# A convolution and attention block on one core: softmax without a shift, with a checked sum and a shifted pass behind a branch

## The chip, the core and the metric

The kernel runs on one core of one Trainium2 chip. Time is the device time of one execution in microseconds (us). Engines are named as the profile names them: PE (TensorE), DVE (VectorE), ACT (ScalarE), POOL (GpSimd), SP (SyncE, which here issues transfers).

## What is computed

Four images of 384 channels and 48 x 48 pixels (N = 2304 tokens) pass through one block, in float32:

```
local = batch_norm(depthwise_conv_7x7(x))
x_norm = layernorm(x tokens)
q, k, v = split(x_norm @ qkv_w.T + qkv_b)         # 8 heads of width 48
q = q + layernorm(local tokens)
attn = softmax(q @ k.T * 48 ** -0.5)
out = x + (attn @ v) @ proj_w.T + proj_b
```

The weights of qkv are normal with variance 1/384; all gains are 1 and all biases 0.

## The kernel before

**Tiles.** An image's tokens form 6 groups (g) of 384, that is 8 image rows or 3 blocks of 128. The 8 heads form 4 pairs (p). In a pair the even head lies on partitions 0 to 47, the odd one on 64 to 111. Row 48 (112) of a query tile holds minus the maximum of that query's scores and row 48 of a key tile holds 1, so the score product, over 49 rows, gives shifted scores.

**Attention** (`attention`, L399) takes one pair of one group of queries and walks over 18 blocks of 128 keys. For each: two score products into `s` (L423, two buffers of PSUM), one exponential of 128 x 768 on ACT into `pt` (L431, three buffers), and, one step later, two products with the values into the accumulator `o` (L409). The values carry a column of ones, so `o` holds the sum of the weights in one more row. There is one buffer for `o`. At the end of the pair ACT and then DVE copy its two halves to `osb` (L442, L443, two buffers), and the next pair can't write `o` until both have.

**Maxima** (`max_part`, L292). The maximum has to be there before the scores are shifted, so while a pair is attended to, the next pair's scores are computed a first time: 36 products of 128 queries by 384 keys (L301), each reduced by DVE to one maximum a query (L309), then a transpose (L314) and two small transfers into row 48 of the query tile (L319). `attention` pulls one step of it a key block. The first pair of an image has its maxima made before its loop.

**Work in between.** Everything else is written as generators whose steps are taken from a queue, `behind`, by `advance(units)` after each key block, five steps at a time. At p = 0 of a group the next group's `q_part` is appended: 147 convolution taps on DVE (L258 and L262, three chunks of 128 channels, each tap a multiply-add onto `acc`, which has one buffer), two layer norms (transposes on PE L145 and L183, statistics L149 and L150, a power on POOL L153, the scaling L157, copies on ACT), four query projections (L199) and four joins with the local part (L280, L285). Behind a pair follows `pair_output` (L335 transposes, L341 reciprocal of the sum, L342 quotient), behind a group `group_output` (L356, L366 projection, L373 residual, then the transfer out). `finish()` empties the queue; it is called before the last pair of a group, as the next group's maxima need its queries. In the last group of an image the queue also gets the first key/value part (`kv_part`: L145, L183, L199, L221) and the first queries of the next image; the other five key/value parts stand between the images, followed by `finish()`.

**Order.** The text is only a priority. A scheduler lays each engine's instructions in one fixed order by a model of their times, and fills an engine's free time with what comes later in the text if its inputs are there. On the chip each engine then goes through its list in that order.

Of the kernel before, what the change touches and what calls it, by code (L numbers as in the profile page):

```python
# [11 lines left out]
ALU = mybir.AluOpType  # L12
AX = mybir.AxisListType

P = 128
NH = 8  # heads
HD = 48  # head width
KS = 7  # convolution window
LN_EPS = 1e-6
BN_EPS = 1e-5  # L20
RG = 8  # image rows in a token group
AHEAD = 1  # key/value groups of the next image that are made ahead


# Two heads share a tile: the even one lies on partitions 0..47 and the odd one on 64..111.
# Row 48 (112) is one more term of the score product: 1 on the key side, minus the row's
# maximum on the query side, so that the product is already the shifted score.
@with_exitstack
def conv_attention(
    ctx: ExitStack,  # L30
    tc: tile.TileContext,
    x: bass.AP,  # [B, C, N]
    conv_w: bass.AP,  # [128, CC, 49]
    bn: bass.AP,  # [128, 4, CC] gamma, beta, mean, var
    ln: bass.AP,  # [128, 2, CC] gamma, beta
    ln_pair: bass.AP,  # [2, 48, 2, 4]
    qk_b: bass.AP,  # [2, 48, 2, 4]
    v_b: bass.AP,  # [1, C]
    qkv_wT: bass.AP,  # [C, 3C]
    proj_wT: bass.AP,  # [C, C]  # L40
    proj_b: bass.AP,  # [128, CC]
    out: bass.AP,  # [B, C, N]
):
# [4 lines left out]
    CC = C // P  # L48
    G = RG * W  # tokens of a group
    NG = N // G  # L50
    NB = G // P  # blocks of 128 tokens in a group
    NP = NH // 2
    KB = N // P
    SCALE = float(HD) ** -0.5
    HA = HD + 1
    KP = 64 + HA

    const = ctx.enter_context(tc.tile_pool(name="const", bufs=1))
# [8 lines left out]

# [1 line left out]
    x_tiles = {}  # L69
# [31 lines left out]
    for j in range(2):  # L101
# [3 lines left out]
        nc.scalar.dma_start(out=qkb[r + HD : r + HA, 1, :], in_=ones)  # L105
    # The query's bias takes the local term's beta as well.
    nc.vector.tensor_add(qkb[:, 0, :], qkb[:, 0, :], ln_p[:, 1, :])
# [14 lines left out]

    # The batch norm goes into the convolution's weights and a shift.
    inv = const.tile([P, CC], F32, tag="inv", name="inv")
# [8 lines left out]

# [1 line left out]
    def normalized(src, dst):  # L135
        """src(c, blk): channels by tokens. dst(blk): where a block's normalized tokens go,
        [128 tokens, heads, 48]."""
        xt = work.tile([P, NB, C], F32, tag="xt", name="xt")
# [28 lines left out]
    def x_normalized(b, g):  # L167
        """The layer norm of x, channels by tokens."""
        xs = x_tiles[b]
# [65 lines left out]

    # The centre of the window is first, as it alone covers every pixel.
    taps = sorted(range(KS * KS), key=lambda t: t != KS * KS // 2)
# [54 lines left out]
    def max_part(b, g, p):  # L292
        """Minus the maximum of each row of scores, into the query's last row."""
        q = queries[b, g][p]
# [32 lines left out]
    def pair_output(b, g, p, osb):  # L327
        """Divides by the sums, tokens by channels."""
        if p == 0:
            outputs[b, g] = work.tile([P, NB, NH, HD], F32, tag="ao", name="ao", bufs=1)  # L330
        ao = outputs[b, g]
        tp = psum()
        ot = tp[:, :G].rearrange("p (t h d) -> p t h d", t=NB, h=2)
        for blk in range(NB):
            nc.tensor.transpose(  # L335
                tp[:, blk * P : blk * P + KP],
                osb[0:KP, blk * P : (blk + 1) * P],
                ident[0:KP, 0:KP],
            )
        rden = work.tile([P, NB, 2, 1], F32, tag="rden", name="rden")  # L340
        nc.vector.reciprocal(rden, ot[:, :, :, HD:HA])  # L341
        nc.vector.tensor_mul(  # L342
            ao[:, :, 2 * p : 2 * p + 2, :],
            ot[:, :, :, 0:HD],
            rden.to_broadcast([P, NB, 2, HD]),
        )
        yield
# [32 lines left out]

# [1 line left out]
    behind = deque()  # work to be spread over the attention's loop  # L382

# [15 lines left out]
    def attention(b, g, p, ahead, units):  # L399
        """ahead: the next pair's max_part, or None."""  # L400
        q = queries[b, g][p]
# [16 lines left out]
        for kb in range(KB):  # L418
            s = ps_s.tile([P, 2, 512], F32, tag="s", name="s")
            blk = kb % NB  # L420
            for j in range(2):
                r = 64 * j
                nc.tensor.matmul(  # L423
                    s[:, j, :G],
                    lhsT=keys[b, kb // NB][r : r + HA, p, blk * P : (blk + 1) * P],
                    rhs=q[r : r + HA, :],
                    start=True,
# [24 lines left out]
    for b in range(B):  # L452
        for _ in max_part(b, 0, 0):
            pass
        for g in range(NG):
            for p in range(NP):
                ahead = None
                if p < NP - 1:
                    ahead = max_part(b, g, p + 1)
                elif g < NG - 1:  # L460
                    finish()
                    ahead = max_part(b, g + 1, 0)
# [7 lines left out]
                if p == NP - 1 and g == NG - 2 and b < B - 1:  # L470
                    load_x(b + 1)
                attention(b, g, p, ahead, 5)
        if b < B - 1:
            for ga in range(AHEAD, NG):
                behind.append(kv_part(b + 1, ga))
        finish()


# [49 lines left out]
```

## Time and profile before

| | |
|---|---|
| median of 3 runs | 5941.53 us (5937.75 to 5945.82) |
| span of the profiled execution | 5940.5 us |
| PE, DVE, ACT, POOL busy | 5593.6, 3993.9, 1791.8, 172.9 us |
| max product L301 on PE, reductions L309 on DVE | 1894.3 and 1783.6 us |
| convolution taps L262 on DVE | 1873.0 us |
| mean granted clock of PE | 0.955 |

The profile gives no other time of the profiled execution than its span. A busy time is the time in which at least one instruction of the engine or group ran; matmuls overlap. In a row of the timeline stand start, duration, engine, line, operation, operands and count, and in brackets the idle time before it and what ended it. `x4` in a row of PE is two float32 matmuls, since each is recorded as two instructions. The granted clock is a share of full speed; in this trace it is either 1 or 0.5 at any moment.

### The profile page before, as it was taken

What the parts mean: (1) busy time and instruction counts of PE and PEld (TensorE: products, weight loads), DVE (VectorE), ACT (ScalarE), POOL (GpSimd) and SP (SyncE); (2) the same over time, 40 slices, a digit from 0 to 9 for tenths busy, and PEclk for the clock granted to TensorE, in tenths of its full rate; (3) what the DMA queues carried; (4) which work ended last, traced back from release to release, by engine and by line L of the source; (5) the groups of instructions that cost most, each with busy time, mean ns of one, the idle gap of its engine ahead of it and who ended that gap; (6) DMA issues with size and microseconds to landing.
All of it is one profiled execution on the core that took longest, in us unless ns stands there. A gap on an engine that the chain in (4) does not pass through costs nothing.

```text
span 5940.5 us, 63623 instructions
## 1 busy us (share of the span) xinstructions
PE 5593.6 (94%) x24720; PEld 2349.8 (40%) x24720; DVE 3993.9 (67%) x8263; ACT 1791.8 (30%) x2545; POOL 172.9 (3%) x325
## 2 busy tenths in 40 slices
PE   6999999999899999999989999999998999999999
PEld 4433333334343333333434333333344433333343
DVE  6795786784738668668563866866855487687543
ACT  2123233223222322322322233233332223323333
POOL 1000000000000000000000000000000000000000
PEclk9799999999999999999989999999999999999999
DMA  1000000000000000000000000000000000000000
GB/s 42 1 1 5 5 1 5 5 25 5 5 1 1 5 5 1 5 5 25 5 5 1 1 5 5 1 5 5 25 5 5 1 2 3 5 2 4 5 5 5
DMA packets 21646, 35.33 MB, mean 6 GB/s; under 512 B 8992, under 2 KB 19808, under 8 KB 19808
## 3 DMA queue, kind: packets, MB, share of 16 engines
q1 hardware_dynamic: 13248, 28.61, 1.3%
q10 hardware_dynamic: 8096, 2.65, 0.2%
q8 instruction: 194, 3.18, 0.2%
q14 instruction: 108, 0.88, 0.0%
HBM read 16.80 MB, written 14.16 MB: 5 GB/s over the span
## 4 chain that ended last, share of the span: by engine, by line
PE 58%; DVE 37%; ACT 2%; POOL 2%; issue 1%; DMA 0%; ACTq 0%; DVEq 0%; POOLq 0%
DVE acc L262 22%; PE s L423 16%; PE o L409 15%; PE pm L301 14%; DVE part L309 9%; PE pm L199 6%; PE pm L366 2%; PE pm L221 2%; DVE st L149 2%; POOL rs L153 1%; PE pm L183 1%; DVE osb L443 1%; DVE xt L157 1%; PE pm L145 1%; DVE lt L157 0%
## 5 line engine op out<-in xcount | busy, mean ns | idle before, releaser
L309 DVE TENSOR_REDUCE part<-pm 128x1 f32<-128x384 f32 x3456 | 1783.6, 551 | 1250.8 <-PE pm L301 1243.4
L431 ACT ACTIVATE pt<-s 128x768 f32<-128x768 f32 x1728 | 1398.2, 811 | 3021.2 <-PE s L423 3019.3
L301 PE MATMUL pm<-k,q 48*128 48x384 f32 x6912 | 1894.3, 513 | 55.6 <-DVE part L309 36.9
L262 DVE SCALAR_TENSOR_TENSOR acc<-x,cw,acc 128x368 f32<-128x368 f32 (+9 forms) x3456 | 1873.0, 582 | 21.1
L423 PE MATMUL s<-q,k 49*128 49x384 f32 x6912 | 1662.9, 553 | 2.7 <-DMA q<-negT 2.7
L409 PE MATMUL o<-pt,v 128*49 128x384 f32 x6912 | 1521.0, 518 | 9.6 <-ACT pt L431 9.4
L301 PEld LDWEIGHTS pm<-k,q 48*128 48x128 f32 x6912 | 850.2, 193 | 778.4 <-DVE part L309 315.1
L423 PEld LDWEIGHTS s<-q,k 49*128 49x128 f32 x6912 | 579.4, 192 | 993.3 <-PE pm L301 490.8
L409 PEld LDWEIGHTS o<-pt,v 128*49 128x49 f32 x6912 | 311.4, 124 | 984.6 <-issue 743.3
L199 PE MATMUL pm<-xnT,w_qk 128*128 128x384 f32 x1152 | 443.3, 534 | 17.8 <-DVE part L309 10.1
L199 PEld LDWEIGHTS pm<-xnT,w_qk 128*128 128x128 f32 x1152 | 228.2, 208 | 200.0 <-ACT xnT L186 36.6
L228 DVE TENSOR_TENSOR v<-pm,vb 128x384 f32<-128x384 f32 x72 | 40.1, 557 | 290.2 <-PE pm L221 290.1
L183 PE MATMUL pm<-ident,xt 128*128 128x128 f32 x432 | 96.4, 357 | 124.2 <-DVE xt L157 105.9
L146 ACT COPY xt<-pm 128x384 f32<-128x384 f32 x216 | 96.2, 482 | 237.3 <-PE pm L145 237.0
L373 DVE SCALAR_TENSOR_TENSOR xr<-pm,pb,xr 128x384 f32<-128x384 f32 x72 | 44.5, 618 | 158.6 <-PE pm L366 158.6
L366 PE MATMUL pm<-aoT,w_o 128*128 128x384 f32 x432 | 148.7, 491 | 0.0
L186 ACT ACTIVATE xnT<-pm,ln_sb 128x384 f32<-128x384 f32 x144 | 90.5, 669 | 184.8 <-PE pm L183 184.8
L221 PE MATMUL pm<-w_v,xnT 128*128 128x384 f32 x432 | 143.6, 487 | 0.0
L149 DVE BATCH_NORM_STATS2 st<-xt 128x6 f32<-128x384 f32 x216 | 112.0, 546 | 31.0 <-ACT xt L146 30.9
L183 PEld LDWEIGHTS pm<-ident,xt 128*128 128x128 f32 x432 | 63.6, 177 | 169.4 <-issue 100.3
L206 ACT ACTIVATE q<-pm,qkb 128x384 f32<-128x384 f32 x96 | 55.8, 581 | 203.0 <-PE pm L199 203.0
L443 DVE COPY osb<-o 49x384 f32<-49x384 f32 x96 | 53.8, 561 | 89.6 <-ACT osb L442 88.5
(51 smaller groups left out, 1228.4 us busy)
## 6 DMA issues: line engine op xcount, KB each, us to landing
x<-in_x_dram SPq DMA_DIRECT2D x12, 1152.0 KB
out_dram<-xr SPq DMA_DIRECT2D x72, 192.0 KB
q<-negT SPq DMA_DIRECT2D x192, 1.5 KB
w_qk<-in_qkv_wT_dram ACTq DMA_DIRECT2D x6, 192.0 KB
w_v<-in_qkv_wT_dram ACTq DMA_DIRECT2D x3, 192.0 KB
w_o<-in_proj_wT_dram ACTq DMA_DIRECT2D x3, 192.0 KB
vb<-in_v_b_dram ACTq DMA_DIRECT2D x1, 192.0 KB
cw<-in_conv_w_dram ACTq DMA_DIRECT2D x1, 73.5 KB
```

The costliest lines, as they stand in the source:

```text
L149: nc.vector.bn_stats(st[:, blk, :], xt[:, blk, :])
L183: nc.tensor.transpose(tp[:, blk * P : (blk + 1) * P], kept["xn"][:, blk, c * P : (c + 1) * P], ident)
L199: nc.tensor.matmul(ps[:, :G], lhsT=w_qk[:, c, which, 2 * p : 2 * p + 2, :].rearrange("p h d -> p (h d)"), rhs=xnT[:, c, :], start=c == 0, ...
L221: nc.tensor.matmul(ps[:, :C], lhsT=xnT[:, c, blk * P : (blk + 1) * P], rhs=w_v[:, c, :], start=c == 0, stop=c == CC - 1,)
L262: nc.vector.scalar_tensor_tensor(dst, src, cw[:, c, t : t + 1], dst, ALU.mult, ALU.add)
L301: nc.tensor.matmul(s[:, :G], lhsT=q[r : r + HD, blk * P : (blk + 1) * P], rhs=keys[b, gk][r : r + HD, p, :], start=True, stop=True,)
L309: nc.vector.tensor_reduce(part[:, i, gk : gk + 1], s[:, :G], AX.X, ALU.max)
L366: nc.tensor.matmul(ps[:, :G], lhsT=w_o[:, c, co * P : (co + 1) * P], rhs=aoT[:, c, :], start=c == 0, stop=c == CC - 1,)
L409: nc.tensor.matmul(o[r : r + HA, :G], lhsT=values[b, kb // NB][:, kb % NB, 2 * p + j, :], rhs=pt[:, j, :], start=kb == 0, stop=kb == KB - 1,)
L423: nc.tensor.matmul(s[:, j, :G], lhsT=keys[b, kb // NB][r : r + HA, p, blk * P : (blk + 1) * P], rhs=q[r : r + HA, :], start=True, stop=True,)
L431: nc.scalar.activation(pt, s[:, :, :G], AF.Exp, scale=SCALE)
L443: nc.vector.tensor_copy(osb[64 : 64 + HA, :], o[64 : 64 + HA, :G])
```

## The change

The kernel's body becomes a function, `attention_pass`, that is called twice. The first call has `shifted=False`: the score product runs over 48 rows, no `max_part` exists, and `advance` takes three steps a key block in place of five. Each pair's reciprocals are compared with 1e15 and 1e-15 (two small DVE instructions) and the result is multiplied into a tile `inside`. After the first call the entries of `inside` below 0.5 are counted by a matmul with ones, the count is loaded into a register of each engine, and if it is over 0 the second call runs, which is the kernel before. All constants and weights are loaded anew in the second call. What the diff takes from comments is left out here.

```diff
-def conv_attention(
+def attention_pass(
...
+    shifted: bool,
+    inside=None,
 ):
...
+    HS = HA if shifted else HD
...
         nc.vector.reciprocal(rden, ot[:, :, :, HD:HA])
+        if inside is not None:
+            flat = rden.rearrange("p t h o -> p (t h o)")
+            for bound, op in ((SAFE, ALU.is_le), (1 / SAFE, ALU.is_ge)):
+                nc.vector.scalar_tensor_tensor(inside, flat, bound, inside, op, ALU.mult)
...
-                    lhsT=keys[b, kb // NB][r : r + HA, p, blk * P : (blk + 1) * P],
-                    rhs=q[r : r + HA, :],
+                    lhsT=keys[b, kb // NB][r : r + HS, p, blk * P : (blk + 1) * P],
+                    rhs=q[r : r + HS, :],
...
-        for _ in max_part(b, 0, 0):
-            pass
+        if shifted:
+            for _ in max_part(b, 0, 0):
+                pass
         for g in range(NG):
             for p in range(NP):
                 ahead = None
-                if p < NP - 1:
+                if p == NP - 1 and g < NG - 1:
+                    finish()
+                if shifted and p < NP - 1:
                     ahead = max_part(b, g, p + 1)
-                elif g < NG - 1:
-                    finish()
+                elif shifted and g < NG - 1:
                     ahead = max_part(b, g + 1, 0)
...
-                attention(b, g, p, ahead, 5)
+                attention(b, g, p, ahead, 5 if shifted else 3)
...
+def conv_attention(tc: tile.TileContext, *args):
+    nc = tc.nc
+    with tc.tile_pool(name="keep", bufs=1) as keep:
...
+        attention_pass(tc, *args, shifted=False, inside=inside)
+        nc.vector.tensor_scalar(outside, inside, 0.5, None, ALU.is_lt)
+        with tc.tile_pool(name="ps_f", bufs=1, space=bass.MemoryType.PSUM) as ps_f:
+            count = ps_f.tile([1, 6], F32, tag="count", name="count")
+            nc.tensor.matmul(count, lhsT=ones, rhs=outside, start=True, stop=True)
+            nc.vector.tensor_reduce(total, count, AX.X, ALU.add)
+        nc.vector.tensor_copy(flag, total)
+        n_outside = nc.values_load(flag[0:1, 0:1])
+        with tc.If(n_outside > 0):
+            attention_pass(tc, *args, shifted=True)
```

Line numbers shift: the score product is L435 after (L423 before), the values' product L421 (L409), the taps L269 (L262), DVE's copy of `o` L455 (L443), the quotient L354 (L342), the range check L353 (new).

The order of the instructions moves with it. First PE inside the loop of a pair, before (image 0, group 1, p2; `pm` is a max product, `o` the accumulator, `s` the scores):

```order
L409 MATMUL o_3083<-pt_3271,v0_3_432 49x384 x2
L423 MATMUL s_3294<-q0_1_2_1760,k0_4_515 128x384 x2
L301 MATMUL pm_3299<-k0_0_179,q0_1_3_1771 128x384
L301 MATMUL pm_3302<-k0_0_179,q0_1_3_1771 128x384
L409 MATMUL o_3083<-pt_3284,v0_3_432 49x384 x2
```

Then PE after, from the end of p2 of the same group into p3 (`s_2482` and on are p3's scores, `o_2152` is p2's accumulator, `o_2479` p3's; `osb_1744` and `osb_2153` are the copied accumulators of p0 and p2):

```order
L421 MATMUL o_2152<-pt_2346,v0_5_610 49x384 x2
...
L435 MATMUL s_2482<-q0_1_3_1573,k0_0_189 128x384 x2
L435 MATMUL s_2487<-q0_1_3_1573,k0_0_189 128x384 x2
L435 MATMUL s_2494<-q0_1_3_1573,k0_0_189 128x384 x2
L190 MATMUL pm_2392<-ident_87,xt_2361 128x128 x3
...
L342 MATMUL pm_2452<-ident_87,osb_1744 128x113 x3
...
L342 MATMUL pm_2470<-ident_87,osb_2153 128x113 x3
L421 MATMUL o_2479<-pt_2485,v0_0_190 49x384 x2
L421 MATMUL o_2479<-pt_2490,v0_0_190 49x384 x2
```

In the loop the max products are gone and `s` and `o` alternate. The next group's norms and query projections, which were spread over p1 and p2, stand in one piece between the last product of p2 and the first of p3, with the outputs of p0, p1 and p2 behind them.

DVE between its copies of `o` for p2 and p3, before (same group; `acc` is the convolution's sum, `part` the maxima):

```order
L443 COPY osb_3084<-o_3083 49x384
L262 SCALAR_TENSOR_TENSOR acc_3710<-x0_73,cw_84,acc_3710 128x8x47
L341 RECIPROCAL rden_3388<-pm_3384 128x6
L262 SCALAR_TENSOR_TENSOR acc_3710<-x0_73,cw_84,acc_3710 128x384
L342 TENSOR_TENSOR ao_3149<-pm_3384,rden_3388 128x3x96
L309 TENSOR_REDUCE part_3399<-pm_3400 128x1
L309 TENSOR_REDUCE part_3399<-pm_3403 128x1
...
L443 COPY osb_3392<-o_3391 49x384
```

And after (`inside` is the range check, `ao` the quotients):

```order
L455 COPY osb_2153<-o_2152 49x384
L353 SCALAR_TENSOR_TENSOR inside_58<-rden_2456,inside_58 128x6
L354 TENSOR_TENSOR ao_2451<-pm_2452,rden_2456 128x3x96
...
L353 SCALAR_TENSOR_TENSOR inside_58<-rden_2474,inside_58 128x6
L269 SCALAR_TENSOR_TENSOR acc_2677<-x0_83,cw_94,acc_2677 128x8x46
L269 SCALAR_TENSOR_TENSOR acc_2677<-x0_83,cw_94,acc_2677 128x384
L269 SCALAR_TENSOR_TENSOR acc_2677<-x0_83,cw_94,acc_2677 128x8x47 x2
...
L455 COPY osb_2480<-o_2479 49x384
```

Before, 39 taps and 36 reductions stood there; now 59 taps, six range checks and three quotients. Counted the same way, DVE's list after has 62 taps between the copies of p3 and of the next group's p0 (18 that alternate between two chunks of channels, 44 that follow each other in one chunk), none between p0 and p1, and 26 between p1 and p2. Groups 1 to 3 of an image differ from this by at most 10 taps. In the last image there are no taps from group 4's p2 on, as no further queries are wanted. Between two images the list of PE has 8 to 9 steps of the next image's first pair in among the five key/value parts.

More of the change, by code (lines that the diff above doesn't have):

```diff
@@ L21 @@
 RG = 8
+SAFE = 1e15
 AHEAD = 1
 @with_exitstack
-def conv_attention(
+def attention_pass(
     ctx: ExitStack,
@@ L476, in conv_attention @@
         finish()
+def conv_attention(tc: tile.TileContext, *args):
+    nc = tc.nc
+    with tc.tile_pool(name="keep", bufs=1) as keep:
+        inside = keep.tile([P, 6], F32, tag="inside", name="inside")
+        outside = keep.tile([P, 6], F32, tag="outside", name="outside")
+        ones = keep.tile([P, 1], F32, tag="ones_col", name="ones_col")
+        total = keep.tile([1, 1], F32, tag="total", name="total")
+        flag = keep.tile([1, 1], mybir.dt.int32, tag="flag", name="flag")
+        nc.vector.memset(inside, 1.0)
+        nc.vector.memset(ones, 1.0)
+        attention_pass(tc, *args, shifted=False, inside=inside)
[8 more added lines that the diff above has]
+            attention_pass(tc, *args, shifted=True)
 def kernel(**inputs):
```

## The prediction

> **What bounds the kernel now.** I read the page's engine totals and costliest groups first.
>
> ```profile
> span 5940.5 us, 63623 instructions
> PE 5593.6 (94%) x24720; PEld 2349.8 (40%) x24720; DVE 3993.9 (67%) x8263; ACT 1791.8 (30%) x2545; POOL 172.9 (3%) x325
> ...
> L309 DVE TENSOR_REDUCE part<-pm 128x1 f32<-128x384 f32 x3456 | 1783.6, 551 | 1250.8 <-PE pm L301 1243.4
> L431 ACT ACTIVATE pt<-s 128x768 f32<-128x768 f32 x1728 | 1398.2, 811 | 3021.2 <-PE s L423 3019.3
> L301 PE MATMUL pm<-k,q 48*128 48x384 f32 x6912 | 1894.3, 513 | 55.6 <-DVE part L309 36.9
> L262 DVE SCALAR_TENSOR_TENSOR acc<-x,cw,acc 128x368 f32<-128x368 f32 (+9 forms) x3456 | 1873.0, 582 | 21.1
> ```
>
> PE looks like the bound, and L301 and L309, both of which go, hold 1894 and 1784 us. But these are busy shares, so I asked what one loop step costs. First the timeline of PE in a pair without convolution (x4 is two float32 matmuls, each recorded as two instructions):
>
> ```profile
> 2453.88 0.92 PE L423 MATMUL s<-q,k 49*128 49x384 f32 x4
> 2454.62 0.81 PE L301 MATMUL pm<-k,q 48*128 48x384 f32 x4
> 2455.37 0.85 PE L409 MATMUL o<-pt,v 128*49 128x384 f32 x4
> 2456.15 0.92 PE L423 MATMUL s<-q,k 49*128 49x384 f32 x4
> ```
>
> A step takes 2456.15 - 2453.88 = 2.27 us. The last pair of an image has no maxima to make ahead, so the trace of before already holds the new loop:
>
> ```profile
> 1560.83 0.92 PE L423 MATMUL s<-q,k 49*128 49x384 f32 x4
> 1561.67 0.85 PE L409 MATMUL o<-pt,v 128*49 128x384 f32 x4
> 1562.45 0.92 PE L423 MATMUL s<-q,k 49*128 49x384 f32 x4
> ```
>
> That step takes 1.62 to 1.63 us: only 0.645 us less, not the 1.10 us that L301's busy time gives (1894.3 / 1728). The exponential (0.81 us) fits in. Then the stretches between the ends of four consecutive pairs (group 2 of the second image: p0, p1, p2, p3):
>
> ```profile
> 2162.30:2212.20 49.90, 49.48 (x249) 20.03 (x248) 21.56 (x43) 16.57 (x24) 1.55 (x2) 1.00 0.04 13
> 2212.20:2267.50 55.30, 52.36 (x253) 21.64 (x254) 34.73 (x76) 20.65 (x32) 2.63 (x4) 0.97 0.00 1
> 2267.50:2331.10 63.60, 60.74 (x252) 24.22 (x248) 63.11 (x129) 16.79 (x24) 1.24 (x3) 1.00 0.00 1
> 2331.10:2386.90 55.80, 52.50 (x221) 20.89 (x221) 43.43 (x86) 15.31 (x20) 0.41 (x1) 0.88 0.00 1
> ```
>
> The columns are length, then PE, weight load, DVE, ACT, POOL and the clock. A group takes 224.6 us. Pair p2 is DVE's (63.11 of 63.60): its convolution taps share DVE with 36 reductions, and the max product waits for these. So the group has two bounds, and I cost it pair by pair.
>
> **The change, part by part: a group's four pairs.** The new loop alone needs 18 x 1.63 = 29.3 us a pair. What else must end before the next pair is the copy of the accumulator (one buffer) by ACT and then DVE, and in the new order DVE's copy stands behind taps. How fast taps go, and what such a copy costs, shows in the timelines of DVE and of all engines:
>
> ```profile
> 2290.67 2.12 DVE L262 SCALAR_TENSOR_TENSOR acc<-x,cw,acc 128x360 f32<-128x360 f32 x4
> ...
> 1559.82 15.32 DVE L262 SCALAR_TENSOR_TENSOR acc<-x,cw,acc 128x376 f32<-128x376 f32 x24
> ...
> 1573.43 0.47 ACT L442 COPY osb<-o 49x384 f32<-49x384 f32 x1 [1.00 <-PE o L409]
> 1575.16 0.56 DVE L443 COPY osb<-o 49x384 f32<-49x384 f32 x1
> 1575.78 0.51 PE L335 MATMUL pm<-ident,osb 113*128 113x113 f32 x3 [2.44 <-DVE osb L443]
> ```
>
> Taps that alternate between two channel chunks start 0.51 us apart ((2.12 - 0.59) / 3); taps of one chunk, each waiting for the last, 0.638 (15.32 / 24). ACT's copy was over at 1573.90, DVE's began at 1575.16 behind taps, and PE stood for 2.44 us. This is small here and is what I expect to grow.
>
> Small DVE steps and group output, by the groups and the timeline of PE:
>
> ```profile
> L341 DVE RECIPROCAL rden<-pm 128x6 f32<-128x6 f32 x96 | 16.0, 182 | 5.6 <-PE pm L335 4.7
> ...
> L373 DVE SCALAR_TENSOR_TENSOR xr<-pm,pb,xr 128x384 f32<-128x384 f32 x72 | 44.5, 618 | 158.6 <-PE pm L366 158.6
> ...
> 1576.13 0.82 PE L356 MATMUL pm<-ident,ao 128*128 128x128 f32 x6
> ...
> 1577.52 5.97 PE L366 MATMUL pm<-aoT,w_o 128*128 128x384 f32 x18
> ```
>
> - p3 (copy of p2 to copy of p3): in the new order DVE has 59 alternating taps, 30.2 us (59 x 0.512), seven small steps of 0.18, three products of 288 elements at the taps' rate (0.4) and the copy (0.56): 33.2. PE needs 0.5 for transposes, 3.1 for the four steps of o that stand together, and 13.5 x 1.63 = 22 for the rest, 26 to 27. DVE ends last; PE then stands some 5 us, as it has only 1.2 us of the next scores to do.
> - p0: 18 alternating and 44 chained taps, 9.2 + 28.1, 1.9 for three residual adds, 1 of small steps: 40 on DVE. PE: 29.3, the output's 0.5 + 1.3 + 6.0, and 1.5 of waits: 38.6 at full clock.
> - p1: no taps. 29.3 and 0.6 for the copy: 29.9.
> - p2: the rest of the queries' work, now in one piece (finish is called before p3, and three units a step leave it over). The start-up has the same piece on PE:
>
> ```profile
> 163.74 1.36 PE L145 MATMUL pm<-ident,acc 128*128 128x128 f32 x9
> 164.94 1.28 PE L145 MATMUL pm<-ident,x 128*128 128x128 f32 x9
> 172.71 2.33 PE L183 MATMUL pm<-ident,xt 128*128 128x128 f32 x9 [6.49 <-DVE xt L157]
> ...
> 185.42 0.49 PE L280 MATMUL pm<-ident,lt 128*128 128x128 f32 x3
> ```
>
> 22.2 us, its 6.49 wait included (scores of p3 fill part of that, and are missing from p3 above). With 2 us for two pairs' transposes, a fill of the output buffer and the copy: 29.3 + 22.2 + 2 = 53.5.
>
> The clock comes on top. After the last pair's short waits the windows read:
>
> ```profile
> 5890.15 0.51 PE L335 MATMUL pm<-ident,osb 113*128 113x113 f32 x3 [1.02 <-DVE osb L443]
> 5891.47 3.26 PE L423 MATMUL s<-q,k 49*128 49x384 f32 x8 [0.82 <-DMA q<-negT]
> ...
> 5892.00:5906.00 14.00, 14.00 (x38) 3.98 (x38) 0.00 (x0) 4.05 (x5) 0.00 (x0) 0.52 0.00 1
> 5906.00:5927.00 21.00, 20.87 (x104) 5.85 (x100) 0.00 (x0) 10.54 (x13) 0.00 (x0) 1.00 0.00 1
> ```
>
> Two waits of 1.02 and 0.82 us are followed by 14 us at half clock, then the new loop stays at full clock for 21 us. The p3 row above, 0.88 over 55.8 us, is 13 us at half. I take 10 us at half after each p3 stall: 5 us lost, p0 = 43.6. It can lose 0 (the clock holds) to 14 us (two such stretches in a group).
>
> A group: 43.6 + 29.9 + 53.5 + 33.2 = 160.2, for 224.6.
>
> **The sum.** Up to 185.9 us nothing shrinks. Then 24 x 160.2 = 3845. Group 5 of three images makes a key/value part in p0, and five more parts stand between images:
>
> ```profile
> 1572.49 0.85 PE L409 MATMUL o<-pt,v 128*49 128x384 f32 x4 [0.19 <-ACT pt L431]
> ...
> 1588.95 2.15 PE L183 MATMUL pm<-ident,xt 128*128 128x128 f32 x9 [4.20 <-DVE xt L157]
> 1591.44 9.78 PE L199 MATMUL pm<-xnT,w_qk 128*128 128x384 f32 x24 [0.34 <-ACT xnT L186]
> 1601.05 5.97 PE L221 MATMUL pm<-w_v,xnT 128*128 128x384 f32 x18
> ...
> 1695.53 4.63 PE L301 MATMUL pm<-k,q 48*128 48x384 f32 x17
> ```
>
> A part is 1.3 + 2.2 + 9.8 + 6.0 = 19.3 of PE: 3 x 19.3 = 58. Between images lie 1695.5 - 1573.3 = 122.2 us, 7.8 of it output that p0 holds already; the new order puts 8 to 9 steps of p0 into the waits for the norm (14 us), so 100.5 each, 301. The last image has no convolution to make ahead: its last five pairs lose 6.6 + 5 + 23.6 + 3.3 = 38. The tail:
>
> ```profile
> 5927.06 0.85 PE L409 MATMUL o<-pt,v 128*49 128x384 f32 x4 [0.19 <-ACT pt L431]
> ```
>
> 12.6 us stay. New behind them are a comparison, a count, a copy, a load of the flag on five engines and a jump: no row shows a load or a jump. Five small steps at 0.2 and as many handovers make 2 us at least; at most I give it the whole tail once more, 12.6; I take 8, nearer to the upper end since five engines each fetch the flag and leave their program. It can't gain, as it waits for the last sums. "Advanced Engine Details and Errata" of the Trainium skill (Control Flow Timing) gives about 0.1 us for a compare-and-branch; no run shown here has one, and by it the jump alone would not be seen. The maxima's 192 small DMAs were waited for only in rows like the 0.82 above.
>
> 185.9 + 3845 + 58 + 301 - 38 + 12.6 + 8 = 4372, against the span of 5940.5; the median of the runs, 5941.5, lies 1 us over it, so 4373.
>
> **The rivals.** (1) DVE doesn't hold p3 and p0: p3 is 26.6, p0 38.6, no stall, no lost clock; 11.6 x 24 = 278 less, 4095. For it: DVE has only (3993.9 - 1783.6) / 24 = 92 us of work in 160. Against: the taps' places and the 2.44 us row. 7%. (2) The clock falls further: with the max product gone PE has more gaps, and if it reads 0.83 in p0, p1 and p2, their 122 us at full clock take 147 in place of 127: 20 x 24 more, 4853. For it: 0.52 above; against: 1.00 for 21 us of the same loop. 12%. (3) The clock falls less: one half-speed stretch as long as the stall itself, 3.4 us, so 1.7 us lost a group and 3.3 x 24 = 79 less, 4294. For it: the 4.20 us wait of 1588.95 is followed by nine transposes in 2.15 us, against 1.36 for those of 163.74, and then by work at full pace. Against: the 14 us row. 10%. This is what "TensorE: Matmul & The Clock Gate" of the Trainium skill (Part 1: The HAM clock gate) would have: an idle window of about 3.4 us halves the clock, a busy one restores it; the row of 14 us after waits of 1.02 and 0.82 does not agree. (4) Slower: the flag. One sum outside 1e-15 to 1e15 starts the second pass, which is the old kernel: 4373 + 5941 = 10314. It takes a scaled score beyond 34.5 (the logarithm of 1e15), or a query all of whose scores lie as far below zero. Queries are two normalized vectors added, keys one, through weights of variance 1/384: 48 products spread by 9.8, scaled 1.4, so 34.5 is some 24 spreads away. Only a fault in the check itself, such as a column of it that is never a sum, would do it. 3%.
>
> **How the numbers follow.** My case has 68%: 4373. Its bounds (0 to 14 us of clock a group, p2 2 us either way) are 4205 to 4640. Rival (3) lies inside; leaving out the far parts of (1) and (2), the upper end of the clock's bound and (4), 4210 to 4610 should hold the time 8 times in 10. Faster is my case and (1) to (3): 0.97; slower is (4): 0.03. No case lies within 0.2% (12 us, about what a measurement of this kernel can tell from no change).
>
> **What would show it.** A step of 1.63 us; groups of about 160; in them PE waits at the end of p3 for DVE's copy of o, about 5 us, with half clock behind it; p2 the longest pair; DVE about 2230 us busy; mean clock near 0.94. Wrong would be: p3 and p0 of 27 and 39 (rival 1); half clock inside p1 (rival 2); full clock within 4 us of the stall (rival 3); a max product in the profile at all (rival 4).

## The result, and the profile after

The changed kernel takes 4406.1 us (median of 4 runs, 4405.7 to 4413.3) where the kernel before takes 5939.6 in the same job: the ratio is 0.742, with a 95% interval of 0.7408 to 0.7432. The forecast was 4373, in a range of 4210 to 4610, and its direction and most of its terms held. The profiled execution has a span of 4403.8 us, against the forecast sum of 4372.

The page of the changed kernel, its span, its engine totals and the groups that answer to those shown of before:

```profile
span 4403.8 us, 45704 instructions
PE 4059.2 (92%) x17714; PEld 1551.7 (35%) x17714; DVE 2339.0 (53%) x4908; ACT 1760.3 (40%) x2449; POOL 182.1 (4%) x325
...
L435 PE MATMUL s<-q,k 48*128 48x384 f32 x6912 | 1725.5, 546 | 5.7 <-ACT pt L443 5.7
...
L421 PE MATMUL o<-pt,v 128*49 128x384 f32 x6912 | 1510.4, 517 | 49.7 <-DVE osb L455 36.3
```

Max product and reductions are gone, and TensorE (PE) is still the busiest engine, at 92%. What is new is the releaser in the last row: the loop's second product now waits for VectorE's copy of the accumulator, `osb` (L455). Next the waits of PE, with total, count and longest:

```profile
PE pm L190 <- DVE xt L164: 142.9, 48, 13.5
PE pm L342 <- DVE osb L455: 115.9, 27, 5.7
PE o L421 <- DVE osb L455: 36.3, 12, 6.6
```

The first is the queries' and keys' normalization, and was there before (105.9 us on the old line L183). The second is the forecast stall behind p3: 27 times, 22 of them 4.8 to 5.7 us long. The third was not in the forecast. Where it lies, the four pairs of group 2 of the second image show (the windows view, stretches between the starts of ScalarE's copies of `o`: length, PE, weight load, DVE, ACT, POOL, clock, DMA's share and GB/s):

```profile
1594.40:1639.30 44.90, 39.77 (x176) 14.45 (x178) 41.68 (x76) 16.38 (x22) 1.84 (x2) 0.92 0.04 14
1639.30:1682.20 42.90, 39.62 (x146) 10.96 (x148) 4.32 (x8) 15.00 (x20) 0.00 (x0) 0.76 0.00 0
1682.20:1735.70 53.50, 49.60 (x227) 20.66 (x227) 21.87 (x50) 24.13 (x36) 3.56 (x6) 0.94 0.00 1
1735.70:1763.10 27.40, 27.40 (x137) 8.51 (x139) 27.09 (x62) 12.47 (x16) 0.82 (x2) 1.00 0.00 1
```

p2 is 53.5, as forecast. p1 is 42.9 instead of 29.9, with VectorE (DVE) nearly idle, ScalarE (ACT) and DMA no busier, and the clock at 0.76: TensorE does the same work more slowly. In groups 1 and 4 p1 is 30.3. The timeline of PE at the start of such a p1 (group 3 of the first image) tells how it comes about:

```profile
717.75 1.55 PE L435 MATMUL s<-q,k 48*128 48x384 f32 x6
722.58 0.92 PE L421 MATMUL o<-pt,v 128*49 128x384 f32 x4 [3.27 <-DVE osb L455]
723.43 1.65 PE L435 MATMUL s<-q,k 48*128 48x384 f32 x4
725.01 1.52 PE L421 MATMUL o<-pt,v 128*49 128x384 f32 x4
726.47 1.65 PE L435 MATMUL s<-q,k 48*128 48x384 f32 x4
...
743.22 1.08 PE L421 MATMUL o<-pt,v 128*49 128x384 f32 x4
744.22 0.92 PE L435 MATMUL s<-q,k 48*128 48x384 f32 x4
745.07 0.85 PE L421 MATMUL o<-pt,v 128*49 128x384 f32 x4
745.85 0.92 PE L435 MATMUL s<-q,k 48*128 48x384 f32 x4
```

PE stands 3.27 us for the copy, and from 723.4 to 744 each step takes 3.03 us (726.47 to 729.50 is the next). Then the step is 1.63 (745.85 - 744.22), as read off before. And why the copy is late is in the timelines of PE and of VectorE one pair earlier:

```profile
676.52 0.82 PE L342 MATMUL pm<-ident,osb 113*128 113x113 f32 x3 [5.13 <-DVE osb L455]
...
678.56 1.52 PE L421 MATMUL o<-pt,v 128*49 128x384 f32 x4
...
682.28 5.73 PE L378 MATMUL pm<-aoT,w_o 128*128 128x384 f32 x12
```

```profile
643.04 0.56 DVE L455 COPY osb<-o 49x384 f32<-49x384 f32 x1 [0.25 <-ACT osb L454]
...
675.90 0.56 DVE L455 COPY osb<-o 49x384 f32<-49x384 f32 x1
...
686.11 0.62 DVE L385 SCALAR_TENSOR_TENSOR xr<-pm,pb,xr 128x384 f32<-128x384 f32 x1 [4.33 <-PE pm L378]
...
692.33 29.51 DVE L269 SCALAR_TENSOR_TENSOR acc<-x,cw,acc 128x384 f32<-128x384 f32 x45
721.87 0.56 DVE L455 COPY osb<-o 49x384 f32<-49x384 f32 x1
```

It is a chain. VectorE's copy at the end of p3 is late behind taps (5.13 us); PE's clock halves; the output projection (L378) runs slowly (12 matmuls in 5.73 us, where the prediction's row of L366 has 18 in 5.97); VectorE, in order, stands 4.33 us for it before the residual add, with its taps behind that; so the next copy ends at 722.4, again late; and the clock halves a second time, now for 20.5 us. That last step is not the same each time: eight waits of 3.27 to 3.29 us stand at this place, in groups 2 and 3, and by the trace's clock records four were followed by 20.5 us at half clock, one by 17.1 and three by 3.4.

The tail, by the timeline of all engines:

```profile
4385.24 0.85 PE L421 MATMUL o<-pt,v 128*49 128x384 f32 x4 [0.19 <-ACT pt L443]
...
4395.85 0.14 DVE L509 CAST flag<-total 1x1 int32<-1x1 f32 x1
```

From the last product of `o` (4386.1) to the span's end are 17.7 us, 12.6 before: the flag costs 5.1.

**A ledger for the clock.** While the clock is at half and PE is busy, nearly half of that time is lost (a step took 3.03 us in place of 1.63). So (1 - mean clock) x span is about what a kernel loses, rather too much than too little, since it counts waits at half clock too: 267 us before (0.955 of 5940.5) and 286 after (0.935 of 4403.8). Both kernels lose much the same; by this they would be 5673 and 4118 at full clock. The table gives this for every kernel below but the last, with the pairs of group 2 of the second image (from start to start of ScalarE's copy of `o`, the second one where it makes both) and the ratio to the kernel before of the same job. Time is the median of the runs; clock, loss and rest are those of the profiled execution, which lay 12 us over the median in max_few and 8 in before_act.

| kernel | time, us | ratio (95%) | clock | lost to clock | rest of span | p0 / p1 / p2 / p3 |
|---|---|---|---|---|---|---|
| before | 5939.6 | 1 | 0.955 | 267 | 5673 | 49.8 / 55.3 / 63.6 / 55.9 |
| after | 4406.1 | 0.7420 (0.7408-0.7432) | 0.935 | 286 | 4118 | 45.0 / 42.8 / 53.5 / 27.5 |
| copy_act | 4269.6 | 0.7195 (0.7183-0.7207) | 0.958 | 179 | 4089 | 44.0 / 30.5 / 54.7 / 28.1 |
| taps_alt | 4323.4 | 0.7286 (0.7274-0.7298) | 0.948 | 225 | 4097 | 44.4 / 30.3 / 55.3 / 27.2 |
| copy_taps | 4264.7 | 0.7191 (0.7180-0.7202) | 0.955 | 192 | 4071 | 44.1 / 30.5 / 55.5 / 27.2 |
| copy_taps_late | 4171.4 | 0.7034 (0.7023-0.7045) | 0.969 | 129 | 4038 | 38.2 / 30.5 / 54.6 / 27.2 |
| no_check | 4365.4 | 0.7362 (0.7352-0.7372) | 0.939 | 266 | 4096 | 47.6 / 34.1 / 54.5 / 27.4 |
| dve_load | 4682.6 | 0.7894 (0.7880-0.7907) | 0.900 | 468 | 4213 | 46.0 / 37.3 / 64.0 / 28.4 |
| max_few | 5836.6 | 0.9835 (0.9819-0.9851) | 0.953 | 275 | 5572 | 49.6 / 54.8 / 64.7 / 48.5 |
| product_free | 5835.8 | 0.9850 (0.9834-0.9867) | 0.923 | 449 | 5384 | 49.6 / 54.6 / 54.0 / 61.6 |
| product_act | 5687.3 | 0.9604 (0.9586-0.9622) | 0.938 | 353 | 5333 | 49.6 / 55.9 / 54.6 / 55.7 |
| max_few_act | 5837.9 | 0.9856 (0.9840-0.9873) | 0.955 | 262 | 5571 | 49.6 / 54.9 / 68.7 / 47.4 |
| before_act | 5910.6 | 0.9972 (0.9963-0.9982) | 0.957 | 254 | 5662 | 49.8 / 54.1 / 64.9 / 53.3 |

### The profile page after: what moved, and what is told of

Read it like the earlier page. It is cut to its first block, busy times and chain, and to the rows that moved or that the text cites. A ratio compares the mean times of both kernels' runs of the same rounds, so it can differ in the third digit from the quotient of the medians.

```text
span 4403.8 us, 45704 instructions
## 1 busy us (share of the span) xinstructions
PE 4059.2 (92%) x17714; PEld 1551.7 (35%) x17714; DVE 2339.0 (53%) x4908; ACT 1760.3 (40%) x2449; POOL 182.1 (4%) x325
## 4 chain that ended last, share of the span: by engine, by line
PE 65%; DVE 29%; POOL 3%; ACT 2%; issue 1%; DMA 0%; ACTq 0%; POOLq 0%
DVE acc L269 23%; PE s L435 23%; PE o L421 21%; PE pm L206 10%; PE pm L378 3%; PE pm L228 3%; PE pm L190 2%; DVE st L156 2%; POOL rs L160 1%; PE pm L368 1%; PE pm L152 1%; ACT pt L443 1%; DVE osb L455 1%; PE pm L287 1%; DVE lt L164 1%
## 5 line engine op out<-in xcount | busy, mean ns | idle before, releaser
L443 ACT ACTIVATE pt<-s 128x768 f32<-128x768 f32 x1728 | 1388.8, 810 | 1546.4 <-PE s L435 1505.7
L269 DVE SCALAR_TENSOR_TENSOR acc<-x,cw,acc 128x368 f32<-128x368 f32 (+10 forms) x3456 | 1870.4, 588 | 36.5
L435 PE MATMUL s<-q,k 48*128 48x384 f32 x6912 | 1725.5, 546 | 5.7 <-ACT pt L443 5.7
L421 PE MATMUL o<-pt,v 128*49 128x384 f32 x6912 | 1510.4, 517 | 49.7 <-DVE osb L455 36.3
L435 PEld LDWEIGHTS s<-q,k 48*128 48x128 f32 x6912 | 583.0, 189 | 1070.6 <-issue 1018.2
L421 PEld LDWEIGHTS o<-pt,v 128*49 128x49 f32 x6912 | 310.1, 124 | 984.3 <-issue 887.6
L455 DVE COPY osb<-o 49x384 f32<-49x384 f32 x96 | 53.8, 560 | 939.0 <-ACT osb L454 937.5
L206 PE MATMUL pm<-xnT,w_qk 128*128 128x384 f32 x1152 | 454.0, 546 | 2.9 <-ACT xnT L193 2.9
L190 PE MATMUL pm<-ident,xt 128*128 128x128 f32 x432 | 98.5, 381 | 144.0 <-DVE xt L164 142.9
L378 PE MATMUL pm<-aoT,w_o 128*128 128x384 f32 x432 | 170.0, 546 | 0.0
L342 PE MATMUL pm<-ident,osb 113*128 113x113 f32 x288 | 54.0, 303 | 119.1 <-DVE osb L455 115.9
L213 ACT ACTIVATE q<-pm,qkb 128x384 f32<-128x384 f32 x96 | 55.7, 581 | 227.5 <-PE pm L206 227.5
L190 PEld LDWEIGHTS pm<-ident,xt 128*128 128x128 f32 x432 | 70.3, 191 | 185.1 <-DVE xt L164 103.0
L159 POOL TENSOR_SCALAR rs<-mv 128x3 f32<-128x3 f32 x72 | 28.6, 397 | 2569.3 <-DVE mv L157 2569.3
L378 PEld LDWEIGHTS pm<-aoT,w_o 128*128 128x128 f32 x432 | 90.5, 219 | 68.8 <-issue 31.9
L213 ACT ACTIVATE k<-pm,qkb 128x384 f32<-128x384 f32 x96 | 55.7, 580 | 142.0 <-PE pm L206 142.0
```

Source lines behind the costliest of these rows:

```text
L190: nc.tensor.transpose(tp[:, blk * P : (blk + 1) * P], kept["xn"][:, blk, c * P : (c + 1) * P], ident)
L206: nc.tensor.matmul(ps[:, :G], lhsT=w_qk[:, c, which, 2 * p : 2 * p + 2, :].rearrange("p h d -> p (h d)"), rhs=xnT[:, c, :], start=c == 0, ...
L213: nc.scalar.activation(dst, ps[:, :G], AF.Identity, bias=qkb[:, which, p : p + 1])
L269: nc.vector.scalar_tensor_tensor(dst, src, cw[:, c, t : t + 1], dst, ALU.mult, ALU.add)
L378: nc.tensor.matmul(ps[:, :G], lhsT=w_o[:, c, co * P : (co + 1) * P], rhs=aoT[:, c, :], start=c == 0, stop=c == CC - 1,)
L421: nc.tensor.matmul(o[r : r + HA, :G], lhsT=values[b, kb // NB][:, kb % NB, 2 * p + j, :], rhs=pt[:, j, :], start=kb == 0, stop=kb == KB - 1,)
```

## Experiments: the stalls that are left

**The copy on ScalarE.** In the changed kernel:

```diff
-        nc.vector.tensor_copy(osb[64 : 64 + HA, :], o[64 : 64 + HA, :G])
+        nc.scalar.copy(osb[64 : 64 + HA, :], o[64 : 64 + HA, :G])
```

> The changed kernel with both halves of the accumulator copied by ACT, none by DVE. Theory (DVE's copy, queued behind taps, holds PE at the ends of p3 and p0, and the half clock in p0 and p1 follows from these waits): the waits of 5.1 and 3.3 us go, p0 falls from 45 to 48 us to about 40, p1 is 30 in every group; about 4120 us (4050 to 4250). Rival A (PE and its clock bound the kernel by themselves, whatever DVE does): 4380 to 4410, with the same half clock.

Measured: 4269.6, 136 us less, of which 107 are clock (286 to 179). So the copy was a cause, and rival A falls; but the gain is half of what theory put, and its range (to 4250) was missed by 20. p1 is 30.5 in every group, while p0 stays at 44. PE's waits of this kernel say what is late next:

```profile
PE pm L190 <- DVE xt L164: 137.8, 45, 13.5
PE pm L368 <- DVE ao L354: 75.4, 24, 4.0
```

Once a group PE now stands for the quotient `ao` (L354). The sums lie ready in PSUM, but VectorE reaches the reciprocal and the quotient only when the taps queued ahead of them are done (all engines, group 2 of the first image):

```profile
645.73 0.48 PE L342 MATMUL pm<-ident,osb 113*128 113x113 f32 x3 [0.31 <-issue]
...
650.71 0.18 DVE L348 RECIPROCAL rden<-pm 128x6 f32<-128x6 f32 x1
...
651.41 0.45 DVE L354 TENSOR_TENSOR ao<-pm,rden 128x288 f32<-128x288 f32 x1
...
652.01 0.87 PE L368 MATMUL pm<-ident,ao 128*128 128x128 f32 x3 [3.52 <-DVE ao L354]
```

**Taps that alternate.** The convolution's loops exchanged, so that neighbouring taps write different chunks:

```diff
-        for c in range(CC):
...
-            for t in taps:
...
+        for t in taps:
...
+            for c in range(CC):
```

> The changed kernel with the taps' loop turned inside out (chunk innermost), so that neighbouring taps never wait for each other. Theory (the 44 chained taps at 0.638 us make p0's copy late): p0's DVE list is 5.6 us shorter, the 3.3 us wait at p0's end and the half clock in p1 of groups 2 and 3 go, the 5 us at p3's end stay; about 4310 us (4260 to 4350). Rival A: 4380 to 4410.

Measured: 4323.4, inside the range. p1 is 30.3 in every group but the first (38.5), and the stall at the end of p3 stays:

```profile
PE pm L342 <- DVE osb L455: 110.9, 39, 5.3
...
PE o L421 <- DVE osb L455: 9.9, 4, 6.4
```

The wait on L421 falls from 36.3 to 9.9 us. So the half clock in p1 comes from VectorE being late in p0, not from the loop itself: rival (2) of the prediction, a clock that falls for want of the max product, is refuted as a cause.

**Both together**, the two edits above:

> The changed kernel with both halves of o copied by ScalarE and the taps alternating between the three channel chunks; same numbers out. Theory (the two stalls are different ones: the copy behind taps at the end of p3 and p0, and the residual ahead of 45 chained taps in p0; but with the copy gone from VectorE the quotient is the next to be late, 3.5 us at the start of p0, and alternating taps do not move it): 4230, between 4200 and 4260. Rival A (the gains add: 4406 - 136 - 83 = 4187 or less): below 4195. Rival B (with the copy on ScalarE the taps' pace in p0 is behind other work): 4262 to 4275, as with the copy alone.

Measured: 4264.7. That is rival B (its upper end was 4275, its lower 4262): once ScalarE makes the copy, nobody waits for the taps of p0, and their pace is hidden. The gains of 136 and 83 are two ways around one chain and don't add.

**And the output projection later.** Behind the two edits:

```diff
         if p == NP - 1:
+            behind.append(iter(range(24)))
             behind.append(group_output(b, g))
```

> copy_taps with the group's output projection put 24 units later into the list of work that is spread over the next pair's steps; same numbers out. TensorE then has steps of p0 to do while VectorE's taps end and the quotient is made. Theory (the rest of the loss over 4095, the estimate without stalls, is the wait for the quotient and the half clock behind it, once a group): no PE wait over 2 us on ao between p3 and p0, 24 x (3.5 + 2.5) = 144 less than copy_taps: 4090, between 4050 and 4150. Rival A (the wait moves on, to the queries' normalization or the next copy): within 40 us of copy_taps. Rival B (slower than copy_taps, since the projection now stands where VectorE's residual adds hold up the next pair's work): above it by 20 or more.

Measured: 4171.4, 93 less than copy_taps; 144 were expected, and the range was missed by 21 us. No rival holds either: the wait for the quotient is nearly gone (76.3 to 10.8 us), and did not move on as a wait of that size. The windows of the same group as above:

```profile
1511.20:1549.50 38.30, 37.99 (x176) 13.47 (x175) 38.30 (x78) 16.93 (x25) 4.31 (x2) 1.00 0.05 17
1549.50:1580.00 30.50, 30.04 (x146) 8.88 (x144) 3.38 (x7) 15.43 (x21) 4.39 (x1) 1.00 0.00 1
1580.00:1634.60 54.60, 50.64 (x229) 21.11 (x226) 18.83 (x47) 24.23 (x37) 3.59 (x7) 0.91 0.00 1
1634.60:1661.70 27.10, 26.82 (x135) 8.17 (x133) 26.98 (x60) 12.95 (x17) 0.41 (x1) 1.00 0.00 1
```

p0 has full clock and takes 38.3, p3 takes 27.1: these are the 38.6 and 26.6 that rival (1) of the prediction gave for a VectorE that holds nothing up. What remains below full clock is p2 (0.91), whose piece of norms and projections waits in the row L190. Of the 144 expected, 60 were for the clock and 84 for the waits. By the ledger the clock gave 63 (192 to 129) and the rest 33 (4071 to 4038): of 65 us of waits removed, half came back, part of it in a new wait of 11.4 us for the residual and in p0 of group 5 (61.9 us, 59.9 in copy_taps). This version computes the same as the changed kernel and is the fastest of this study.

## Experiments: what the removed parts had cost

**Few scores in the maxima.** The kernel before, reductions made small:

```diff
-    nc.vector.tensor_reduce(part[:, i, gk : gk + 1], s[:, :G], AX.X, ALU.max)
+    nc.vector.tensor_reduce(part[:, i, gk : gk + 1], s[:, :8], AX.X, ALU.max)
```

> The kernel before, with each maximum taken over 8 of its 384 scores, so that the second score product stays on PE and its 3456 reductions almost vanish from DVE (softmax is the same for any shift). Theory (the gain is two things, a step shorter by 0.645 us on PE and DVE freed in the convolution's pairs): the pairs of p2 and p3 fall to PE's 2.27 us a step; a group near 197, about 5200 us (5050 to 5350). Rival B (PE's product is all that counted): 5800 to 5940. Rival C (DVE's reductions are all that counted): 4400 to 4600.

Measured: 5836.6, and rival B holds: theory missed by over 600 us. 1300 us of VectorE's work went, and p2 did not get shorter. Its windows (the first row is all engines; the second, of another answer, the taps alone):

```profile
2221.50:2286.20 64.70, 61.97 (x252) 24.25 (x250) 64.11 (x151) 16.75 (x24) 1.24 (x3) 1.00 0.00 1
```

```profile
2221.50:2286.20 64.70, 59.19 (x107) 1.00 0.00 1
```

And the taps alone in the same p2 of the kernel before:

```profile
2267.50:2331.10 63.60, 45.33 (x84) 1.00 0.00 1
```

VectorE is still busy for 64.11 of 64.70 us: 107 taps stand in p2, where there were 84. The scheduler filled the room, and the product still waits for VectorE in order; where no reduction reads it (product_free and product_act in the table), p2 takes 54.0 and 54.6. So "p2 is VectorE's" was right, but what made it so was the order of its instructions, not the sum of its work.

**The same load beside the changed loop.** Two reductions a step over constant data, read by nobody:

```diff
+            if not shifted:
+                for j in range(2):
+                    nc.vector.tensor_reduce(
+                        part[:, j, kb % NG : kb % NG + 1], w_v[:, j, :], AX.X, ALU.max
+                    )
```

> The changed kernel with two reductions of 384 values a key block put back on DVE, over a constant tile that nothing waits for: DVE's load of before without the product and without its waits. Theory (DVE's time counts too): DVE then has 92 + 67 = 159 us of work in a group of about 165, its copies come later; about 4900 us (4650 to 5200). Rival B (PE's product is all that counted): under 4500.

Measured: 4682.6, in the range, rival B falls. VectorE is busy for 3846.4 us in place of 2339.0. The reductions' time costs 277 us in the changed kernel, 182 of them clock (286 to 468) and only 95 the rest.

**The product without reductions.** The kernel before, with `part` set to zero and the reductions taken out:

```diff
+        nc.gpsimd.memset(part, 0.0)
...
-                    nc.vector.tensor_reduce(part[:, i, gk : gk + 1], s[:, :G], AX.X, ALU.max)
```

> The kernel before with every max product still on TensorE, but no reduction reading it: VectorE's 3456 reductions are left out, the shift is 0, and its transposes and small DMAs stay. Theory (of the 1431 us that the product still cost beside small reductions, 5837 against 4406, some 1110 are TensorE's own time, 96 pairs x 18 steps x 0.645 us, and the rest is its standing in order for VectorE, of which the small-reduction run shows 245 us in the row 'PEld pm L301 <- DVE part L309'): 5550, between 5400 and 5650, and no wait of PE on the reductions' line. Rival A (the coupling costs nothing, the product's own time is all of it): 5750 to 5860. Rival B (the product alone is cheap, below half of 1431, and the order of waits was the cost): below 5150.

Measured: 5835.8, which reads like rival A, but the run does not isolate what it should. Its row for the end of p2 (timeline of PE, same group) shows a new stall:

```profile
2270.19 0.82 PE L334 MATMUL pm<-ident,osb 113*128 113x113 f32 x3 [16.84 <-DVE osb L442]
```

```profile
PE pm L334 <- DVE osb L442: 310.3, 50, 16.9
```

With nothing to wait for, the taps stand together ahead of the copy, and PE stood 310 us in all for it (the waits of PE, the second fence). Therefore the three kernels that follow move the copy to ScalarE, to be set beside copy_act.

> product_free (the kernel before, max product kept, the 3456 reductions left out, shift 0) with both halves of o copied by ScalarE. In product_free VectorE had nothing to wait for and the taps stood together, 96 of them ahead of the copy at the end of p2, where PE stood 16.8 us (311 us in all, with 17 to 27 us of half clock behind each); so that run didn't isolate the product. To be set beside the changed kernel with ScalarE's copy, 4270. Theory (the product's own price is its 0.645 us in each of 1728 steps, 1115 us): 5385, between 5300 and 5480. Rival A (the product costs more than its time in the step, by small weight loads or a lower clock): 5550 to 5700. Rival B (the copy was not what stood in product_free): 5780 or more.

Measured: 5687.3, 1418 more than copy_act and 302 over theory: rival A's range, and in part its reason, since 174 of these are clock (179 to 353); most of the rest is the wait shown below. p0, where no wait falls, is 49.6 at clock 1.00, and 18 steps of 2.27 with the 7.8 of output are 48.7: the product costs its step there. In p3 it stands, since the PSUM buffer that it needs is held until VectorE has made the quotient behind the taps:

```profile
2216.22 1.65 PE L302 MATMUL pm<-k,q 48*128 48x384 f32 x4 [9.58 <-DVE ao L341]
2217.80 1.52 PE L408 MATMUL o<-pt,v 128*49 128x384 f32 x4
```

In all, by the waits of PE:

```profile
PE pm L302 <- DVE ao L341: 152.3, 19, 11.1
```

Of the 1418, 1115 are the product's steps (1728 x 0.645), 152 this wait and 174 clock (179 to 353): 1441 together, 23 too many.

> The kernel before with maxima over 8 of each 384 scores (the shift leaves the other columns out) and with both halves of o copied by ScalarE. Theory (beside product_act only small reductions are added, so what it takes more is the max product's standing in order for VectorE, 245 us by the waits of the first run with small maxima): 5385 + 245 = 5630, between 5540 and 5720. Rival A (that wait lies beside others and costs little): within 60 of product_act. Rival B (the copy plays no part where reductions pace VectorE): 5800 to 5840.

Measured: 5837.9, rival B; with small reductions the copy's place is worth nothing (5836.6 with VectorE's copy). It takes 151 more than product_act. Since product_act has a stall that this kernel lacks, the small reductions and the product's waiting for them should cost at least that; how much more was not isolated.

> The kernel before with both halves of o copied by ScalarE, nothing else changed; same numbers out. Tells how much of the change's gain is bound up with the copy. Theory (the copy's wait at pair ends in the kernel before is about 2.4 us with some half clock, in up to three of four pairs, but p2 is held by VectorE): 5820, between 5740 and 5890, so that 5820 to 4270 is the price of product and reductions with that stall gone from both. Rival A (no part of the bound): 5915 to 5940. Rival B (it gives as much as in the changed kernel, 136 or more): 5800 or less.

Measured: 5910.6, ratio 0.9972 (0.9963 to 0.9982): a gain of 16 us, between the ranges of theory and rival A. The edit that is worth 136 us in the changed kernel is worth 16 before: the copy's wait became a bound by the change.

With the copy on ScalarE throughout, the way from before to after is 5911 to 5838 (short reductions: 73) to 5687 (none: 151) to 4270 (no product: 1418). The last step also leaves out the product's transposes and small transfers and changes the order of the work in between (three units a step in place of five); what these do to the 1418 was not isolated.

## Experiments: what was added

**Without tests, flag and second pass:** `conv_attention` calls `attention_pass(tc, *args, shifted=False)` and nothing else.

> The changed kernel without the range tests of the sums, without flag and branch: one pass without a shift, the second pass left out of the program. Theory (the tail's 5.1 us go, and with them the 192 tests, 30 us of VectorE, of which the six in p3 and two in p0 lie ahead of copies that TensorE waits for: 24 x 1.2 = 29 at most): 4380, between 4365 and 4398. Rival A (only the tail is on the path): 4399 to 4403. Rival B (the second pass in the program costs more than the tail shows, code loading or scheduling): below 4360.

Measured: 4365.4, at the lower edge of the range; 41 less than the changed kernel. Its tail is 12.5 us, so 5.2 are the flag's, and 20 more are clock (286 to 266). The eight waits at the end of p0 in groups 2 and 3 are 2.5 us here, in place of 3.3, and are followed by 3.4 to 10.2 us at half clock, in place of 3.4 to 20.5. The small tests of p3 and p0, which stand ahead of the copies for which PE waits, fit that; that it was they, and not some other change of order, was not shown, and the other 16 us were not taken apart.

**The flag taken:** `SAFE = 1.0`, so that the sums lie outside and the second pass runs.

> The changed kernel with the tests' bounds both at 1, so that nearly every sum lies outside, the flag is set and the second pass with maxima runs behind the first. Theory (the branch works as written and the second pass is the kernel before, constants and start-up included): 4406 + 5940 = 10346, between 10250 and 10420. Rival A (the second pass overlaps the tail or finds its program and constants at hand): below 10250. Rival B (loading the second program after the jump stalls the engines): above 10420.

Measured: 10343.5 in one run, theory's 10346 within 3 us. So the prediction's price for rival (4), 10314, was nearly right; it didn't come about, as the changed kernel's profile has no second pass. The handover, by the timeline of all engines:

```profile
4409.96 0.14 DVE L509 CAST flag<-total 1x1 int32<-1x1 f32 x1
4410.91 0.21 POOL masks.py:197 MEMSET ident<- 128x128 f32 x1 [70.00 <-DVE flag L509]
```

The second pass's first instruction starts 0.81 us after the flag is written (4410.91 - 4410.10). The changed kernel, which leaves that pass out, ends 7.8 us after its flag (4403.8 - 4395.99). "Advanced Engine Details and Errata" of the Trainium skill (Control Flow Timing) gives a compare-and-branch about 0.1 us. In the changed kernel's own trace four engines' branches took under 0.08 us, and PE's took 4.3. Its rows of the flag's load (L510) and of the branch (L511) give minimum, median and longest in ns (`PEldq` is PE's sequencer, `ACTq` ScalarE's):

```profile
L510 DVEq TENSOR_LOAD <-flag x1: 547/547/547, 4396.0 to 4396.0; - x1
```

```profile
L511 ACTq COMPARE_BRANCH  x1: 54/54/54, 4396.6 to 4396.6; - x1
...
L511 PEldq COMPARE_BRANCH  x1: 4335/4335/4335, 4396.6 to 4396.6; - x1
...
L511 ACTq EVENT_SEMAPHORE  x1: 17/17/17, 4400.1 to 4400.1; - x1
```

The load takes about 0.5 us on each engine. ScalarE's branch takes 0.05 us, but its next instruction starts only 3.5 us later, and PE's branch takes 4.3 us. In the run with the flag taken, where the second pass follows at once, PE's longest branch takes 0.18 us. So most of the 5.1 us lies in the jump over the second pass, and not in loading the flag; what the engines wait for in it the trace doesn't say.

## Why the prediction was right, and where it was off

- **The loop step** (1.63 for 2.27): right, 1.63 in the rows above. The prediction took 0.645 us a step from the last pair of an image rather than 1.10 from the product's busy time, and that term, 1115 us, is the largest one that the runs confirm.
- **p2 in one piece**, 53.5: right, 53.4 to 54.9 in groups 0 to 3 and 51.6 in group 4 (57.7 in group 5). The key/value part beside group 5, 160.2 + 19.3 = 179.5: measured 179.7, but with p0 at 64.4, p2 at 57.7 and p3 at 27.2, so that part of this agreement is luck. Image boundaries with their group, 160.2 + 100.5 = 260.7: measured 257.0.
- **The stall behind p3**, "some 5 us": right, 5.13 in the row, 115.9 us in all. By VectorE's copies p3 took 32.9 us (643.04 to 675.90) where 33.2 stood; by ScalarE's, p3 and p0 together take 72.4 to 76 in groups 1 to 4, where 33.2 + 43.6 = 76.8 stood.
- **The clock behind that stall**, "10 us at half": right, 6.8 or 10.2 after 20 of the 22 long waits. Rival (3), one stretch of 3.4 us, came after the other two.
- **p0, the step that failed.** The text set 40 us of VectorE beside 43.6 of PE and let VectorE finish first. The 40 held work alone. VectorE stood 4.33 + 0.42 us for the output projection, which the half clock of p0 itself had slowed, and all 45 taps of the last chunk were behind that wait. From one copy to the next it took 46 us (675.90 to 721.87), and PE waited.
- **p1**, 29.9: right where p0's copy was in time (30.3 in groups 1, 4 and 5), wrong in groups 2 and 3 (34.9 to 42.9, by p0's late copy and the half clock behind it). Over the whole run this is 88 us more (with 13.5 in the first group); the other terms gave 56 back on balance, and the sum came out 32 too low. That it lies so near is in part luck. Half clock inside p1 was named as the sign of rival (2). The sign came; its cause is the wait, as taps_alt shows.
- **The flag**, 8: 5.1 us, inside its bounds of 2 and 12.6. The reason given, that five engines each fetch the flag and leave their program, was right for the leaving; the fetch takes 0.5.
- **VectorE**, "about 2230 us busy": 2339. Its busy time counts overlapping instructions once, so taking 1783.6 off it took too much: the kernel before without reductions (product_free) still has 2333.4. Without the tests (no_check) it is 18 less.
- **Mean clock**, "near 0.94": 0.935, though of the 286 us lost only 24 x 5 = 120 stand in the sum as a term of their own.
- **"Two bounds"**: the prediction held p2 to be VectorE's for its work. max_few shows that work to be movable: a third of VectorE's time went and 2% of the kernel's.

## What to carry to other kernels

Cost a step to be removed by what the loop's period loses where the trace already shows it without that step, not by its busy time; and when an in-order engine is given a time, add its waits for the engine that you are costing, since a stall that slows that engine comes back to it. Where a scheduler places the work, a load that is taken off is refilled from the next one: look at the order before reading an experiment as an isolation. A short copy that frees a single buffer belongs on the engine with the shortest queue, here ScalarE, and its price can be small before a change (16 us) and large after it (136 us).

## What the runs showed of the hardware

- A wait of 3.27 us was followed by 20.5 us at half clock, with PE at work back to back all that time (723.4 to 744). A wait of the same length at the same place in another group was followed by 3.4. The stretches at half clock in the changed kernel are, by the trace's clock records, 3.4, 6.8, 10.2, 17.1 or 20.5 us long, multiples of 3.4. "TensorE: Matmul & The Clock Gate" of the Trainium skill (Part 1: The HAM clock gate) has a window of about 3.4 us, and full clock after at least one busy window: the multiples agree with such a window, and "at least one" is up to six here. What sets their number was not settled.
- In copy_taps a copy of 1152 elements on GpSimd (POOL), begun while VectorE ran alternating taps, ended 1 us after that run of taps (timeline):

```profile
1557.70 20.61 POOL L250 COPY xr<-x 128x1152 f32<-128x1152 f32 x1 [18.55 <-DMA out_dram<-xr]
1559.69 17.62 DVE L269 SCALAR_TENSOR_TENSOR acc<-x,cw,acc 128x376 f32<-128x376 f32 x34
```

Of its 24 copies there 16 took 14.8 to 20.6 us and the others 1.1 to 1.6; in copy_act all took 1.1 to 1.4. Nobody waited for it in either. Why was not settled.
